# A four-layer fp32 kernel: in the last layer, image 0's depthwise convolution moved from TensorE to VectorE, setup work reordered, and another access pattern for the column products

## The chip, the core and the metric

The kernel runs on one core of a Trainium2 chip. The core has a matrix engine (TensorE, "PE" in the profile; its weight loads are "PEld"), a vector engine (VectorE, "DVE"), a scalar engine (ScalarE, "ACT"), a general engine (GpSimd, "POOL") and a queue engine that issues the DMAs used here (SyncE, "SP"). Compute tiles lie in SBUF, matmul results in PSUM, which this kernel treats as eight "banks" of 512 fp32 values per partition.

The metric is the device time of one execution in microseconds. The time before is the median of three runs. The profile is of one more execution; the span in it goes from the first to the last instruction.

## What is computed

Four layers follow one another on four images of 192 channels and 56 x 56 pixels, all in fp32. Only the last is touched. For each image it does, cut down:

```python
xn = layer_norm(x)                                # over channels
xc, z = split(in_proj_w @ xn)                     # 192 channels each
xc = silu(depthwise_conv3x3(xc, conv_w) + conv_b) # "u" in the kernel
xs = [rows(xc), columns(xc), reversed rows, reversed columns]
dts, Bv, Cv = split(x_proj_w[k] @ xs[k])          # 12 + 4 + 4 values per pixel, 4 directions
dt = softplus(dt_proj_w[k] @ dts + dt_proj_b)
h[t] = exp(dt*A) * h[t-1] + dt*Bv*xs              # a scan of 3136 pixels, 4 states per channel
y = sum over directions of (h . Cv) + Ds * xs
out = x + out_proj_w @ (layer_norm(y) * silu(z))
```

The first and third directions walk the image along rows, the second and fourth along columns, so the products `x_proj_w @ xs` are needed once in row order and once in column order.

## The kernel before

`layer3` is the last layer. Channels are held as two halves of 96 partitions, and an image as seven chunks of 448 pixels (eight rows). Tiles that feed matmuls have 128 partitions, and partitions 96 to 127 hold zeros. Its parts, by name:

- **Setup** (lines 1688 to 1753). Weights are loaded, the input bias is formed by 16 small matmuls (L1695) and copied (L1702), and the projection weights are scaled on DVE (L1704). An identity is made on POOL, and from it 18 diagonal matrices of 96 x 96, one for each tap of the 3 x 3 convolution and each half (L1722, DVE). `keep` allocates the working tiles and, where asked, zeroes partitions 96 to 127 on POOL (L1732): two u tiles, y, two pads, four rows, two sq; the dr tiles are zeroed whole (L1740). This part is placed by the framework's own scheduler.
- **`begin(b, c)`** starts chunk c of image b: loads x (L1803), prepares the borders of a padded tile on POOL (L1809 to L1815), normalizes (`layer_norm`: matmul L1768, DVE L1770, ACT square L1778, matmul L1783, ACT L1786 and L1787, DVE L1789), projects with matmuls (L1821) and writes the pad on ACT (L1832). The convolution then runs on PE: nine matmuls per half, each with one diagonal as weights and a shifted window of the pad as input, summed in a bank (L1851), and copied with its bias to u by ACT (L1859). The gate is projected and copied (L1868), both get SiLU (L1873, L1874), and `product` forms the row product. A chunk's pad work waits until the chunk before has its pad, and until the chunk before last is convolved.
- **`product`** is two matmuls into a bank (L1893), a copy by ACT (L1896) and a store (L1899). `begin_columns` calls it once per chunk of columns when all rows of the image are done, and there it reads u at a stride of 56 values: consecutive matmul columns are consecutive rows of the image.
- **`load`, `sizes`, `decay`, `scan`** do a step of 448 pixels of one direction. In `scan`, per half: DVE forms du (L2046 in row order, L2049 in column order), PE spreads it (L2056), DVE multiplies (L2062, three) and scans (L2078, three), POOL multiplies the states by C (L2085), PE sums over states (L2101), and DVE adds into y (L2106, L2111, L2115). L2115 reads the bank at a stride of 56 values and y in runs of eight.
- **`final(b, c)`** normalizes y, gates, projects and stores.

The order of these instructions on PE, DVE, ACT and POOL is fixed when the kernel is built: `Order.run` holds all the generators as threads, each with a place, and repeatedly takes the operation that could start first by assumed costs (`on_pe`, `on_dve`, ...), plus 0.05 times its place. Image 0's chunks have places -52 + 6c, steps have about 2t. A thread may yield a condition, and then it waits until the condition holds. Each engine runs its list strictly in order.

A fp32 matmul shows in the profile as two records. The third layer (`layer2`) has depthwise convolutions of its own, on DVE: one `tensor_scalar` and eight `scalar_tensor_tensor` operations per half (L1341, L1343).

Of the kernel before, what the change touches and what calls it, by code (L numbers as in the profile page):

```python
# [240 lines left out]
class Order:  # L241
# [20 lines left out]
    def take(self, kind="bank"):  # L262
        slot = min((s for s in self.kinds[kind] if s[0] is not None), key=lambda s: s[0])
        slot[0] = None
        return slot[1]

    def done(self, tile):

        (slot,) = (s for slots in self.kinds.values() for s in slots if s[1] is tile)
        slot[0] = self.end + self.LATENCY  # L270
# [66 lines left out]
def on_act(*n, takes=(), table=None, ready=None):  # L337
    return "ACT", sum(0.2 + 0.0009 * i for i in n), takes, table, ready
# [1337 lines left out]
def layer3(tc, src, packs, aps, dst):  # L1676
# [8 lines left out]
    with ExitStack() as ctx:  # L1685
# [28 lines left out]
        nc.vector.memset(eps, EPS)  # L1714

        ident = const.tile([HALF, HALF], F32, name="c_ident")
        make_identity(nc, ident)
        diag = const.tile([128, 2, 9, HALF], F32, name="diag")
        nc.gpsimd.memset(diag[HALF:], 0.0)
        for h in range(2):  # L1720
            for t in range(9):
                nc.vector.tensor_scalar_mul(diag[:HALF, h, t], ident, w["c96.conv_w"][:, h, t : t + 1])  # L1722

        per = ctx.enter_context(tc.tile_pool(name="c_per", bufs=1))
        ps = ctx.enter_context(tc.tile_pool(name="c_ps", bufs=1, space=PSUM))

        def keep(name, shape, n, rows=128, zero=True):

            tiles = [per.tile([rows, *shape], F32, name=f"{name}{i}") for i in range(n)]
            if zero:  # L1730
                for t in tiles:
                    nc.gpsimd.memset(t[HALF:], 0.0)  # L1732
            return tiles

        us = keep("u", [2, HW], 2)
        (y,) = keep("y", [2, HW], 1)
        pads = keep("pad", [2, 11, W + 2], 2)
        drs = keep("dr", [SCH], 3, zero=False)
        for t in drs:
            nc.gpsimd.memset(t, 0.0)  # L1740
        order = Order(
            nc,
            bank=[ps.tile([128, 512], F32, name=f"c_bank{i}") for i in range(8)],
            row=keep("row", [2, CH], 4),
            sq=keep("sq", [2, CH], 2),
            gate=keep("gate", [2, CH], 2, HALF, False),
            prod=keep("prod", [512], 2, 40, False),
            dr=drs,
            bc=keep("bc", [SCH], 8, zero=False),
            dt=keep("dt", [SCH], 6, HALF, False),  # L1750
            du=keep("du", [SCH], 3, HALF, False),
            da=keep("da", [SCH], 10, zero=False),
            st=keep("st", [SCH], 12, zero=False),
        )
        take, done = order.take, order.done
        prods = [[dram.tile([40, HW], F32, name=f"prod{b}_{o}") for o in range(2)] for b in range(B)]
# [35 lines left out]
        def begin(b, c):  # L1792


            u = us[b % 2]

            yield lambda: (b, c) == (0, 0) or (gone("begun", b, c - 1) if c else gone("begun", b - 1, NCHUNK - 1))
            yield lambda: b < 2 or gone("scanned", b - 2)

            yield lambda: b == 0 or gone("multiplied", 8 * NSC * (b - 1) + 4 * c)  # L1800
            yield on_sp("row", "row")
            xl, xn = take("row"), take("row")
            nc.sync.dma_start(xl[:HALF], pixels(src[b])[:, :, c * CH : (c + 1) * CH])  # L1803

            i = NCHUNK * b + c
            pad, above = pads[i % 2], pads[(i - 1) % 2]
            yield lambda: i < 2 or gone("convolved", i - 2)
            yield on_pool(200, 200)
            nc.gpsimd.memset(pad[:HALF, :, :, 0 : W + 2 : W + 1], 0.0)  # L1809
            if c == 0:  # L1810
                nc.gpsimd.memset(pad[:HALF, :, 1], 0.0)
            else:
                nc.gpsimd.tensor_copy(pad[:HALF, :, 0:2, 1 : 1 + W], above[:HALF, :, 8:10, 1 : 1 + W])
            if c == NCHUNK - 1:
                nc.gpsimd.memset(pad[:HALF, :, 10], 0.0)  # L1815
            yield from layer_norm(xl, xn, over=(xl,))

            def project(m):
                px = take()
                for k in range(2):  # L1820
                    nc.tensor.matmul(  # L1821
                        px[:HALF, :CH], inT[:, k, HALF * m : HALF * m + HALF], xn[:, k], start=(k == 0), stop=(k == 1)
                    )
                return px

            tiles = []
            for m in range(2):
                yield on_pe(2 * CH, "bank")
                tiles.append(project(m))
            for m in range(2):  # L1830
                yield on_act(CH)
                nc.scalar.activation(  # L1832
                    pad[:HALF, m, 2:10, 1 : 1 + W],
                    rows2(tiles[m][:HALF, :CH]),
                    AF.Identity,
                    bias=in_b[:, m : m + 1],
                )
                done(tiles[m])
            passed.add(("begun", b, c))
            y0, y1 = max(8 * c - 1, 0), 8 * c + (8 if c == NCHUNK - 1 else 7)  # L1840
            n = y1 - y0
            at = y0 - (8 * c - 1)
            px = slice(y0 * W, y1 * W)
            zt = None
            for h in range(2):
                pz = pc = None
                for t in range(9):
                    yield on_pe(n * W, *(("bank",) if t == 0 else ()), ready=order.end - 0.5 if t else None)
                    if t == 0:
                        pc = take()  # L1850
                    nc.tensor.matmul(  # L1851
                        rows2(pc[:HALF, : n * W]),
                        diag[:, h, t],
                        pad[:, h, at + t // 3 : at + t // 3 + n, t % 3 : t % 3 + W],
                        start=(t == 0),
                        stop=(t == 8),
                    )
                yield on_act(n * W)
                nc.scalar.activation(  # L1859
                    u[:HALF, h, px], pc[:HALF, : n * W], AF.Identity, bias=w["c96.conv_b"][:, h : h + 1]  # L1860
                )
                done(pc)
                yield on_pe(2 * CH, "bank")
                pz = project(2 + h)
                yield on_act(CH, takes=() if h else ("gate",))
                if h == 0:
                    zt = take("gate")
                nc.scalar.activation(zt[:, h], pz[:HALF, :CH], AF.Identity, bias=in_b[:, 2 + h : 3 + h])  # L1868
                done(pz)
            done(xn)  # L1870
            passed.add(("convolved", i))
            yield on_act(2 * n * W, 2 * CH, table=SILU)
            nc.scalar.activation(u[:HALF, :, px], u[:HALF, :, px], AF.Silu)  # L1873
            nc.scalar.activation(zt, zt, AF.Silu)  # L1874
            yield on_sp()
            nc.sync.dma_start(pixels(zmem[b])[:, :, c * CH : (c + 1) * CH], zt)
            done(zt)
            yield from product(b, 0, px, u[:, :, px], 2)
            passed.add(("rows", b, c))

        def begin_columns(b, c):
            yield lambda: all(gone("rows", b, i) for i in range(NCHUNK))
            uv = us[b % 2].rearrange("p h (y x) -> p h x y", x=W)[:, :, 8 * c : 8 * c + 8]
            yield from product(b, 1, slice(c * CH, (c + 1) * CH), uv, 4)
            passed.add(("columns", b, c))

        def product(b, o, px, u, passes):

            n = px.stop - px.start
            yield on_pe(passes * n, "bank")  # L1890
            pp = take()
            for k in range(2):
                nc.tensor.matmul(pp[:40, :n], w["c128.xpT"][:, k, o], u[:, k], start=(k == 0), stop=(k == 1))  # L1893
            yield on_act(n, takes=("prod",))
            t = take("prod")
            nc.scalar.copy(t[:, :n], pp[:40, :n])  # L1896
            done(pp)
            yield on_sp()
            nc.sync.dma_start(prods[b][o][:, px], t[:, :n])  # L1899
            done(t)  # L1900
# [225 lines left out]
        for b in range(B):  # L2126
            for c in range(NCHUNK):
                order.add(n * (b - 1) + 6 * c + 4, begin(b, c))
                order.add(n * (b - 1) + 48 + c, begin_columns(b, c))
                order.add(n * (b + 1) - 2 * c, final(b, c))  # L2130
        for t in range(len(steps)):
            order.add(2 * t - 5, load(t))
            if t % 2 == 0:
                order.add(2 * t - 3, sizes((t, t + 1)))
            for h in range(2):
                order.add(2 * t + h - 1, decay(t, h))
                order.add(2 * t + h, scan(t, h))
# [35 lines left out]
```

## Time and profile before

| what | value |
|---|---|
| median of three runs | 6957.4 us (6956.57 to 6957.86) |
| the profiled execution's own time | 6951.71 us |
| its span | 6949.9 us |
| mean granted PE clock | 0.931 of full speed |
| PE busy | 5890.7 us (85%) |
| DVE busy | 5908.5 us (85%) |
| ACT busy | 2640.6 us (38%) |
| POOL busy | 1423.8 us (20%) |
| last layer's first weight load is issued | at 4901.8 us |

A group line of the profile names the line, the engine, the operation, its output and inputs with sizes, and the count; after the bar come busy microseconds and the mean nanoseconds of one; after the next bar the engine's idle time before these instructions and what ended it. In the chain of waits, each line has a start, a length, and the work on the chain. In the table by stage, "granted clock" is the share of full speed that PE was given. A busy engine is only a bound where the others wait for it, so the last layer is read stage by stage below.

### The profile page before, as it was taken

The numbers are of one execution on the slowest core, as the hardware profiler recorded it, in microseconds if no ns is written. First come the engines' busy times: TensorE is split into PE (matmuls) and PEld (weight loads), VectorE is DVE, ScalarE is ACT, GpSimd is POOL, SyncE is SP. The second block draws the span as 40 slices with busy tenths as digits, with TensorE's granted clock in tenths as the row PEclk, the third lists the DMA queues.
The fourth block names the chain that finished last, engine by engine and source line by source line (L and its number), as shares of the span: only waits on it lengthen the run. The fifth ranks groups of instructions, "written<-read, shape, count | busy, mean of one in ns | idle before, by whom it ended". The sixth has DMA issues, their size and how long they took to land. (4 is left out here: it accounts for less than half of the span.)

```text
span 6949.9 us, 107660 instructions
## 1 busy us (share of the span) xinstructions
PE 5890.7 (85%) x43810; PEld 2685.0 (39%) x43810; DVE 5908.5 (85%) x7379; ACT 2640.6 (38%) x4083; POOL 1423.8 (20%) x1409
## 2 busy tenths in 40 slices
PE   4999979999999994968888787885799989899776
PEld 2445434444444441345444444442332222222211
DVE  2799999999999999648999898997348788887897
ACT  1111112221122211135555455543256656556543
POOL 0000000000000000032222222220125445445564
PEclk9999989999999997979999899987899999999998
DMA  3222112221222112110000000000145555555654
GB/s 94 56 52 64 34 35 53 58 65 35 52 64 61 35 45 73 45 52 16 19 19 14 19 17 17 19 14 8 34 104 130 142 143 129 152 133 136 166 151 108
DMA packets 252044, 462.69 MB, mean 67 GB/s; under 512 B 30388, under 2 KB 237964, under 8 KB 240412
## 3 DMA queue, kind: packets, MB, share of 16 engines
q1 hardware_dynamic: 251548, 455.80, 25.8%
q8 instruction: 345, 5.65, 0.3%
q14 instruction: 151, 1.24, 0.1%
HBM read 238.58 MB, written 62.96 MB: 43 GB/s over the span
## 5 line engine op out<-in xcount | busy, mean ns | idle before, releaser
L789 DVE TENSOR_TENSOR pr<-vdx,attn 112x1792 f32<-112x1792 f32 (+4 forms) x720 | 1185.6, 1648 | 19.0
L634 PE MATMUL a_bank<-qk_in,w_a 64*49 64x392 f32 x9408 | 1156.3, 496 | 0.0
L2085 POOL TENSOR_TENSOR da<-st,bc 128x448 f32<-128x448 f32 x672 | 859.0, 1283 | 862.9 <-DVE st L2078 618.9
L794 DVE TENSOR_TENSOR oa<-oa,pr 112x1792 f32<-112x1792 f32 (+1 forms) x423 | 764.8, 1808 | 0.0
L634 PE MATMUL a_bank<-qk_in,wd 64*49 64x392 f32 x4032 | 689.6, 493 | 0.0
L2078 DVE TENSOR_TENSOR_SCAN st<-da,st,c_bank 128x448 f32<-128x448 f32 x576 | 646.6, 1132 | 0.0
masks.py:197 POOL MEMSET b_ident<- 128x128 f32 x1 | 0.2, 205 | 2856.0 <-DVE sc L1042 2856.0
L634 PEld LDWEIGHTS a_bank<-qk_in,w_a 64*49 64x49 f32 x9408 | 431.6, 120 | 394.1 <-issue 389.2
L2062 DVE TENSOR_TENSOR c_bank<-c_bank,bc 128x448 f32<-128x448 f32 x672 | 382.5, 618 | 153.1 <-PE c_bank L2056 152.5
L315 ACT ACT_TABLE_LOAD x378 | 485.0, 1283 | 6.6
L2031 ACT ACTIVATE da<-da,a_neg 128x448 f32<-128x448 f32 x672 | 414.1, 658 | 122.5 <-DMA da<-dt 117.9
L1343 DVE SCALAR_TENSOR_TENSOR bg<-bzpad,w_b,bg 128x448 f32<-128x448 f32 (+2 forms) x672 | 423.1, 684 | 0.0
L2101 PE MATMUL c_bank<-da,w_c 128*32 128x448 f32 x1344 | 349.5, 570 | 66.3 <-POOL da L2085 61.4
L1851 PE MATMUL c_bank<-pad,diag 128*96 128x448 f32 (+2 forms) x1008 | 396.8, 543 | 2.4 <-ACT pad L1832 2.3
L794 DVE TENSOR_TENSOR ob<-ob,pr 112x1792 f32<-112x1792 f32 (+3 forms) x282 | 393.0, 1394 | 0.0
L2056 PE MATMUL c_bank<-du,w_c 32*128 32x448 f32 x1344 | 257.8, 624 | 121.6 <-DVE du L2046 80.4
L869 PE MATMUL a_bank<-xc,w_a 128*128 128x448 f32 x672 | 296.8, 571 | 66.0 <-DVE xc L854 66.0
L878 ACT ACTIVATE hm<-a_bank,w_a 128x448 f32<-128x448 f32 x168 | 106.4, 634 | 637.4 <-PE a_bank L869 618.3
L634 PEld LDWEIGHTS a_bank<-qk_in,wd 64*49 64x49 f32 x4032 | 247.4, 119 | 256.5 <-issue 254.6
L1432 PE MATMUL bank<-bxn,w_b 128*128 128x448 f32 (+2 forms) x672 | 288.1, 557 | 24.8 <-DVE bxn L1215 18.6
L884 PE MATMUL a_bank<-hm,w_a 128*96 128x448 f32 x672 | 290.6, 564 | 21.3 <-ACT hm L878 21.3
L655 PE MATMUL a_bank<-qk_sum,w_a 64*49 64x168 f32 (+1 forms) x5376 | 277.7, 337 | 27.1 <-DVE qk_sum L625 25.2
(305 smaller groups left out, 9825.2 us busy)
## 6 DMA issues: line engine op xcount, KB each, us to landing
da<-dt SPq DMA_DIRECT2D x672, 224.0 KB
vdx<-vmem SPq DMA_DIRECT2D x168, 476.0 KB
bc<-prod SPq DMA_DIRECT2D x224, 224.0 KB
row<-x SPq DMA_DIRECT2D x56, 336.0 KB
x<-x SPq DMA_DIRECT2D x4, 2352.0 KB
vmem<-vt SPq DMA_DIRECT2D x56, 168.0 KB
xc<-x SPq DMA_DIRECT2D x56, 168.0 KB
mid<-xc SPq DMA_DIRECT2D x56, 168.0 KB
```

The costliest lines, as they stand in the source:

```text
L315: self.nc.scalar.preload_act_table_set(table)
L634: nc.tensor.matmul(py[a][outs[g], : 7 * W].rearrange("p (y x) -> p y x", x=W), wt[halves[a], dx], q[halves[a], r, i0 + m : i0 + m + 7, dx ...
L789: nc.vector.tensor_mul(pr, vv, wt)
L794: nc.vector.tensor_add(og, og, before)
L869: nc.tensor.matmul(ph[:, :CH], w["a128.c1T"][:, k, 128 * m : 128 * m + 128], xt[:, k], start=(k == 0), stop=(k == 1),)
L1343: nc.vector.scalar_tensor_tensor(dst, x, wt[:, t : t + 1], dst, ALU.mult, ALU.add)
L1851: nc.tensor.matmul(rows2(pc[:HALF, : n * W]), diag[:, h, t], pad[:, h, at + t // 3 : at + t // 3 + n, t % 3 : t % 3 + W], start=(t == 0), ...
L2031: nc.scalar.activation(da, da, AF.Exp, scale=a_neg[:, k, g : g + 1])
L2062: nc.vector.tensor_mul(tiles[j][:, :SCH], tiles[j][:, :SCH], b_)
L2078: nc.vector.tensor_tensor_scan(sts[j][:, r], da[:, r], tiles[j][:, :SCH][:, r], first, ALU.mult, ALU.add)
L2085: nc.gpsimd.tensor_mul(da, sts[j], c_)
L2101: nc.tensor.matmul(py[32 * j : 32 * j + 32, :SCH], w["c128.sum"], das[j], start=True, stop=True)
```

## The change

Five things change, all in `layer3`:

1. Image 0's convolution is done on DVE: per half, one `tensor_scalar` (tap 0 times weight, plus bias) and eight `scalar_tensor_tensor` operations that add a tap each, straight into u. Its matmuls and the ACT copy with bias are not issued. Images 1 to 3 keep the matmuls.
2. The 18 diagonals are built by a thread of their own, `diagonals`, with place 0, once the row product of image 0's fourth chunk has been placed; later images' convolutions wait for it, in the written order.
3. The zeroing is shared: the row, sq and pad tiles are zeroed on DVE; u, dr, the diagonals' lower rows and y on POOL, in that order, with the identity made after dr.
4. The column products read u in image-row order: for each row, eight neighbouring values. The result is written to the bank at a stride of 56 values, so the bank's content is laid out as before.
5. The planner's cost of a column product goes from 4 to 2 passes.

```diff
+        rows = keep("row", [2, CH], 4, zero=nc.vector)
+        sqs = keep("sq", [2, CH], 2, zero=nc.vector)
+        pads = keep("pad", [2, 11, W + 2], 2, zero=nc.vector)
+        us = keep("u", [2, HW], 2, zero=nc.gpsimd)
+        drs = keep("dr", [SCH], 3)
         for t in drs:
             nc.gpsimd.memset(t, 0.0)
+        make_identity(nc, ident)
+        nc.gpsimd.memset(diag[HALF:], 0.0)
+        (y,) = keep("y", [2, HW], 1, zero=nc.gpsimd)
...
-                pz = pc = None
-                for t in range(9):
+                pz = pc = uh = None
+                if b == 0:
+
+                    for t in range(9):
+                        yield on_dve(n * W, each=0.0012, ready=order.end - 0.3 if t else None)
+                        v = pad[:HALF, h, at + t // 3 : at + t // 3 + n, t % 3 : t % 3 + W]
+                        uh = rows2(u[:HALF, h, px])
+                        wt = w["c96.conv_w"][:, h, t : t + 1]
+                        if t == 0:
+                            nc.vector.tensor_scalar(uh, v, wt, w["c96.conv_b"][:, h : h + 1], ALU.mult, ALU.add)
+                        else:
+                            nc.vector.scalar_tensor_tensor(uh, v, wt, uh, ALU.mult, ALU.add)
+                if uh is None:
+                    yield lambda: gone("diagonals")
+                for t in range(9 if uh is None else 0):
...
-                yield on_act(n * W)
-                nc.scalar.activation(
-                    u[:HALF, h, px], pc[:HALF, : n * W], AF.Identity, bias=w["c96.conv_b"][:, h : h + 1]
-                )
-                done(pc)
+                if uh is None:
+                    yield on_act(n * W)
...
+        def diagonals():
+
+            yield lambda: gone("rows", 0, 3)
+            for h in range(2):
+                for t in range(9):
+                    yield on_dve(HALF)
+                    nc.vector.tensor_scalar_mul(diag[:HALF, h, t], ident, w["c96.conv_w"][:, h, t : t + 1])
+            passed.add(("diagonals",))
+
         def begin_columns(b, c):
             yield lambda: all(gone("rows", b, i) for i in range(NCHUNK))
-            uv = us[b % 2].rearrange("p h (y x) -> p h x y", x=W)[:, :, 8 * c : 8 * c + 8]
-            yield from product(b, 1, slice(c * CH, (c + 1) * CH), uv, 4)
+            uv = us[b % 2].rearrange("p h (y x) -> p h y x", x=W)[:, :, :, 8 * c : 8 * c + 8]
+            yield from product(b, 1, slice(c * CH, (c + 1) * CH), uv, 2)
...
+            out = pp[:40, :n].rearrange("p (x y) -> p y x", y=H) if o else pp[:40, :n]
             for k in range(2):
-                nc.tensor.matmul(pp[:40, :n], w["c128.xpT"][:, k, o], u[:, k], start=(k == 0), stop=(k == 1))
+                nc.tensor.matmul(out, w["c128.xpT"][:, k, o], u[:, k], start=(k == 0), stop=(k == 1))
...
+        order.add(0, diagonals())
```

More of the change, by code (lines that the diff above doesn't have):

```diff
@@ L1716, in layer3, with keep @@
         ident = const.tile([HALF, HALF], F32, name="c_ident")
-        make_identity(nc, ident)
         diag = const.tile([128, 2, 9, HALF], F32, name="diag")
-        nc.gpsimd.memset(diag[HALF:], 0.0)
-        for h in range(2):
-            for t in range(9):
-                nc.vector.tensor_scalar_mul(diag[:HALF, h, t], ident, w["c96.conv_w"][:, h, t : t + 1])
         per = ctx.enter_context(tc.tile_pool(name="c_per", bufs=1))
         ps = ctx.enter_context(tc.tile_pool(name="c_ps", bufs=1, space=PSUM))
-        def keep(name, shape, n, rows=128, zero=True):
+        def keep(name, shape, n, rows=128, zero=None):
             tiles = [per.tile([rows, *shape], F32, name=f"{name}{i}") for i in range(n)]
@@ L1731, in keep @@
                 for t in tiles:
-                    nc.gpsimd.memset(t[HALF:], 0.0)
+                    zero.memset(t[HALF:], 0.0)
             return tiles
[L1735 to L1738, printed above, removed]
+        rows = keep("row", [2, CH], 4, zero=nc.vector)
[3 more added lines that the diff above has]
+        drs = keep("dr", [SCH], 3)
         for t in drs:
             nc.gpsimd.memset(t, 0.0)
+        make_identity(nc, ident)
+        nc.gpsimd.memset(diag[HALF:], 0.0)
+        (y,) = keep("y", [2, HW], 1, zero=nc.gpsimd)
         order = Order(
@@ L1743, in layer3 @@
             bank=[ps.tile([128, 512], F32, name=f"c_bank{i}") for i in range(8)],
[L1744 to L1747, printed above, removed]
+            row=rows,
+            sq=sqs,
+            gate=keep("gate", [2, CH], 2, HALF),
+            prod=keep("prod", [512], 2, 40),
             dr=drs,
[L1749 to L1753, printed above, removed]
+            bc=keep("bc", [SCH], 8),
+            dt=keep("dt", [SCH], 6, HALF),
+            du=keep("du", [SCH], 3, HALF),
+            da=keep("da", [SCH], 10),
+            st=keep("st", [SCH], 12),
         )
@@ L1845, in begin @@
             for h in range(2):
-                pz = pc = None
-                for t in range(9):
+                pz = pc = uh = None
[12 more added lines that the diff above has]
+                for t in range(9 if uh is None else 0):
                     yield on_pe(n * W, *(("bank",) if t == 0 else ()), ready=order.end - 0.5 if t else None)
@@ L1857, in begin @@
                     )
-                yield on_act(n * W)
-                nc.scalar.activation(
-                    u[:HALF, h, px], pc[:HALF, : n * W], AF.Identity, bias=w["c96.conv_b"][:, h : h + 1]
-                )
-                done(pc)
+                if uh is None:
+                    yield on_act(n * W)
+                    nc.scalar.activation(
+                        u[:HALF, h, px], pc[:HALF, : n * W], AF.Identity, bias=w["c96.conv_b"][:, h : h + 1]
+                    )
+                    done(pc)
                 yield on_pe(2 * CH, "bank")
```

## The prediction

> **What bounds the kernel now.** I read five views in this order. First the page's engine totals: TensorE 85% and VectorE 85% of the span, so neither is the bound throughout and the stages must be looked at apart. Second, busy time by stage of the last layer:
>
> ```profile
> 4904.00:4940.00 36.00, 11.76 (x29) 5.81 (x30) 26.09 (x25) 4.93 (x7) 25.82 (x17) 0.55 0.19 56
> 4942.00:5118.00 176.00, 173.38 (x475) 68.53 (x474) 26.78 (x32) 81.30 (x113) 10.67 (x20) 1.00 0.23 61
> 5118.00:5153.00 35.00, 32.78 (x62) 6.43 (x63) 17.14 (x22) 12.48 (x18) 10.84 (x9) 0.95 0.25 70
> 5153.00:6455.00 1302.00, 1175.09 (x3843) 363.63 (x3844) 1039.09 (x1341) 787.08 (x1123) 631.75 (x521) 0.96 0.55 138
> 6455.00:6950.00 495.00, 349.79 (x1098) 90.31 (x1097) 438.80 (x565) 239.37 (x350) 273.42 (x208) 0.89 0.54 141
> ```
>
> After the stage and its length come the busy microseconds of PE, its weight loads, DVE, ACT and POOL, then PE's granted clock. While image 0 is begun (4942 to 5118) PE is busy 98% and DVE 15%. From 5153 to 6455, where each image's scans run beside the next image's convolution, PE has 90%, DVE 80%. The last image's scans are DVE's (89%). Third, the chain of waits:
>
> ```profile
> 4904.00 10.70 POOL u L1732 x2
> 4914.70 5.38 POOL y L1732
> 4924.15 3.74 POOL row L1732 x4
> 4927.89 1.60 POOL sq L1732 x2
> ...
> 5003.19 6.77 PE c_bank L1851 x18
> 5009.95 4.51 PE c_bank L1821 x12
> 5014.46 6.06 PE c_bank L1851 x16
> 5020.52 1.63 PE c_bank L1893 x4
> ...
> 5129.79 23.19 PE c_bank L1893 x28
> ```
>
> Three things lead to image 0's scans: POOL's zeroing (L1768 starts at 4926.24, during the row memsets), the convolution L1851, about 13.7 of each chunk's 25.3 us (L1768 starts at 4972.50, 4997.78, 5023.07), and the column products: seven take 23.19 us, 3.31 each, where a row product takes 1.63 for the same 448 columns. Fourth, the groups by line give DVE's prices (busy total, mean):
>
> ```profile
> L1343 DVE SCALAR_TENSOR_TENSOR bxn<-bapad,w_b,bxn 96x448 f32<-96x448 f32 x320 | 207.6, 689 | 0.0
> L1341 DVE TENSOR_SCALAR bxn<-bapad,w_b 96x448 f32<-96x448 f32 x40 | 19.1, 516 | 0.0
> L2111 DVE TENSOR_TENSOR y<-y,c_bank 96x448 f32<-96x448 f32 x56 | 34.0, 607 | 14.8 <-PE c_bank L2101 14.5
> L2115 DVE TENSOR_TENSOR y<-y,c_bank 96x448 f32<-96x448 f32 x112 | 68.1, 608 | 93.7 <-PE c_bank L2101 93.5 <-ACT da L2031 0.2
> ```
>
> L1343 and L1341 are layer 2's own depthwise convolution, the same operations on windows of the same shape. Fifth, the timeline of 4904 to 5160, for starts and ends.
>
> **Part 1, the start.** Removed ahead of L1768: 18 diagonal products on DVE (21.04 us at 4904, stretched by POOL: the longest, 5.41, has the length of a u memset) and POOL's memsets of y, pad, row and sq ahead of or in the way of the first chunk. Added on DVE: the row, sq and pad memsets, 3.74 + 1.60 + 2.44 = 7.8 us by POOL's rows. DVE is free from 4901.8 and L1712 took its 0.14 us inside a POOL memset, so I expect no stretching: done by 4912. Then L1768 waits for PE's own queue: the bias products L1695 end at 4913.0, after the weights land at 4910.2. L1768 at 4913.0 against 4926.24: **-13 us**. POOL keeps u 10.70, dr 1.53, identity 0.43, diag 1.53, y 5.38 = 19.6, to 4923.6; the pad edges behind them (0.5) end at 4924.1, ahead of the first pad write at 4939.93 - 13 = 4926.7. That cover is 2.6 us; what exceeds it comes on the path. L1704's two products can be held by u's memset to 4914.7; needed at 4924. SP's queue is unchanged; the first rows were loaded by 4912.
>
> **Part 2, image 0's convolution.** PE loses 14 half-chunks, 7 x 13.7 = 96 us, all on the chain; ACT loses 14 L1859 copies (0.63 each, 9 us, hidden). DVE gains 14 x (0.52 + 8 x 0.64) = 79 us; 0.64 lies between L1343's start-to-start 0.60 and mean 0.69. Behind each such instruction queue the next chunk's L1770 and L1789, for which PE's L1783 and L1821 wait: one operation, 0.6 us a time. Summing DVE's work until the state that before has at 5153:
>
> - convolution 79; the norms of six chunks and of image 1's first (L1770 and L1789): 7 x 2.15 = 15;
> - the five half-steps of scans done by then: each du 0.6, three multiplications 1.7, three scans 3.3, one sum 0.67, about 6.5, so 33;
> - the diagonals, now after image 0's fourth chunk: 18, between 0.15 (estimate from 96 elements at L1711's rate) and 1.2 each (L1722 under POOL). POOL is then mostly idle; I take 0.4, 7 us.
>
> That is 134 us. The first pad is ready at 4940.6 - 13 = 4927.4, so a DVE that never idles ends at 5061. It will idle: a chunk's chain of L1768, L1770, L1778, L1783, L1786, L1789, L1821, L1832 took 11.8 us unloaded (4972.5 to 4984.3), may start only when the chunk before last is convolved, and the last image-0 chunk is followed by SiLU and its product (4 us) before any column product. L2046, which like L1343 reads two tiles of SBUF, has a mean of 0.846 against 0.589 at best while POOL is half busy; here POOL has 15 products of 1.28 in some 130 us, so perhaps 0.08 for each of 112 operations, 9 us, of which 0.64 holds 4. For all this I allow 10%, 13 us: 5074, or 79 us earlier than 5153. The column products of image 0 (Part 3) run beside this DVE work on an otherwise light PE, so their own saving is partly in it; I add 5. Parts 1 and 2: **-84 us** (bounds -100, DVE never idle, and -45, the slower chunk of rival B).
>
> Later images: their convolution stays on PE and additionally waits, in the written order, for the diagonals. They are queued near 5000 to 5040, image 1's convolution follows after 5050: nothing. The new condition shifts the planner's places a little; +-10 us in the range.
>
> **Part 3, column products.** Their input u is now read in runs of eight contiguous values, the bank is written at a stride of 56 values. If the read alone sets the price, a product falls from 3.31 to 1.63: 1.68 x 21 = 35 us of PE for images 1 to 3. PE is 90% busy there and DVE fell to 37 of 50 us in the windows with the products (40 elsewhere), so I take 70%: **-24 us**. The trace has no matmul with a strided bank. The nearest row is L2115 against L2111: DVE reads the bank at just this stride and y in just these runs, and pays 0.608 against 0.607. [...] The bounds are 1.63 and, a guess with no row behind it, 8. I take the row, because a matmul here delivers a value per 0.84 ns and record and DVE drew strided ones at 1.36 ns: at that pace a product would still cost only 2.4.
>
> **Sum.** -84 - 24 = -108 against the profiled execution's 6951.71 (span 6949.9 and 1.8 around it): 6844. The timed median, 6957.4, is 5.7 higher, so **6850**.
>
> **Rivals.**
> A. *The bank's stride eats the column gain* (3.31 as before): 6850 + 29 = 6879. [...]
> B. *Image 0's chunks are bound by the chain, not by DVE's work.* PE will now have gaps. At the start, 33% busy, it had a clock of 0.55, and L1768, L1783 and L1821 took 3.27, 3.18 and 4.94 instead of 1.67, 1.74 and 3.2: 4.8 us a chunk, 29 us for six chunks, plus 10 for DVE's order: 6889. [...]
> C. *Slower.* The strided bank costs far more than the strided read. With A and Parts 1 and 2 the gain left is 79; each extra microsecond per product costs 7 + 0.7 x 21 = 22 us, so it decides from 3.31 + 3.6 = 6.9 us per product on; at 8 it is 6980. L2115 speaks against; nothing in the trace excludes it.
> D. *No change*: the planner's new order loses in 5153 to 6455 what the start gained, because both PE and DVE are near full. Against: the order there comes from the same costs, except for the columns. 6957.
>
> **How the numbers follow.** Chances: forecast 0.62, A 0.13, B 0.13, C 0.07, D 0.05. The forecast's own range is 6815 to 6880 (DVE never idle and all 35 us: 6957 - 16 - 11 - 108 = 6822; the planner's 10 below). A and B reach to about 6905. I give 6810 to 6905, which leaves C, D and some tails out. A measurement of this kernel tells 0.2%, 14 us: faster 0.88 (forecast, A, B), same 0.04, slower 0.08.
>
> **What would show it.** L1768 first at about 4913; the first L1832 near 4927; some 126 DVE operations of 0.5 to 0.65 us on u, DVE about 90% and PE about 75% busy to 5050; chunks 15 to 17 us apart instead of 25; L1893 at 0.41 us a record for columns as for rows; the first image-1 convolution some 80 us earlier; PE's busy sum some 140 us lower. Wrong would be: L1893 records of 0.8 us or more, PE's clock below 0.8 in that stage, or a distance from the first image-1 convolution to the end that has grown.

## The result

| | before | after |
|---|---|---|
| median of five runs, us | 6957.86 (6956.57 to 6960.48) | 6850.14 (6844.28 to 6855.94) |
| ratio | | 0.9845 (95%: 0.9831 to 0.9858) |
| profiled execution, its span | 6951.71, 6949.9 | 6850.6, 6848.8 |
| last layer in it | 2048.5 | 1939.8 |

"Last layer" runs from its first instruction on DVE, the memset of c_ones at L1711, to the end. The layers ahead of it, which the change doesn't touch, took 4901.4 us in one profile and 4909.1 in the other, so below the last layer is compared by times counted from that memset. It is 108.8 us shorter. In the changed kernel the convolution's lines on DVE are L1855 (first tap) and L1857 (the other eight), PE's convolution is L1864, the product L1918 (before: L1893), and the zeroing L1727.

| us after that memset | before | after | gained so far |
|---|---|---|---|
| first mean, L1768 on PE | 24.9 | 11.9 | 13.0 |
| first subtraction, L1770 on DVE | 28.2 | 24.0 | 4.2 |
| first pad write, L1832 on ACT | 38.5 | 33.6 | 4.9 |
| last column product of image 0, its end | 251.6 | 192.0 | 59.6 |
| first convolution matmul of image 1 | 258.5 | 198.9 | 59.6 |
| end | 2048.5 | 1939.8 | 108.8 |

So 60 us come before image 1's convolution and 49 behind it. The page's engine totals of the changed kernel:

```profile
PE 5770.1 (84%) x43558; PEld 2650.3 (39%) x43558; DVE 5982.6 (87%) x7513; ACT 2621.1 (38%) x4063; POOL 1409.3 (21%) x1401
```

Busy time by stage of its last layer, with the columns as before (stage, length, then busy time of PE, weight loads, DVE, ACT and POOL, then PE's granted clock):

```profile
4942.00:5060.00 118.00, 88.85 (x208) 30.52 (x206) 97.83 (x149) 68.93 (x93) 9.47 (x16) 0.88 0.30 81
5100.00:5400.00 300.00, 278.68 (x949) 91.44 (x947) 233.84 (x301) 185.49 (x264) 144.06 (x121) 0.99 0.54 131
5400.00:6360.00 960.00, 842.28 (x2882) 267.00 (x2882) 798.44 (x1034) 592.27 (x852) 484.87 (x399) 0.96 0.58 145
6360.00:6850.00 490.00, 358.65 (x1114) 92.58 (x1112) 438.66 (x571) 237.86 (x350) 274.87 (x209) 0.89 0.56 145
```

While image 0 is begun, DVE is busy 83% and PE 75%: neither is full, and PE's clock fell from 1.00 to 0.88. Images 1 and 2 (5400 to 6360) have PE at 88% and DVE at 83%. The chain of waits in the first stage shows one chunk, and then the column products:

```profile
4949.26 1.09 DVE row L1770
4950.36 0.96 ACT sq L1778
4951.37 3.30 PE c_bank L1783 x4
4954.67 2.39 PE c_bank L1821 x4
4957.73 1.28 ACT L315
4959.03 0.86 ACT u L1887
4959.88 0.84 ACT gate L1888
4961.89 0.79 DVE u L1857
4967.60 1.09 DVE row L1770
...
5090.38 10.65 PE c_bank L1918 x28
```

From one L1770 to the next the chain runs through the norm and the projection, past a table load and both SiLUs on ACT, into one half's taps. The seven column products take 10.65 us where they took 23.19.

### The profile page after: what moved, and what is told of

Its sections match the earlier page's. It is cut to its first block, busy times and chain, and to the rows that moved or that the text cites. A ratio compares the mean times of both kernels' runs of the same rounds, so it can differ in the third digit from the quotient of the medians.

```text
span 6848.8 us, 107270 instructions
## 1 busy us (share of the span) xinstructions
PE 5770.1 (84%) x43558; PEld 2650.3 (39%) x43558; DVE 5982.6 (87%) x7513; ACT 2621.1 (38%) x4063; POOL 1409.3 (21%) x1401
## 4 chain that ended last, share of the span: by engine, by line
DVE 49%; PE 35%; issue 7%; ACT 5%; DMA 2%; POOL 2%; SPq 0%; DVEq 0%; POOLq 0%; ACTq 0%
DVE pr L789 9%; DVE oa L794 7%; PE a_bank L634 6%; DVE bg L1343 5%; DVE ob L794 4%; PE c_bank L1864 4%; DVE st L2103 3%; DVE bxn L1343 3%; PE c_bank L1821 2%; PE a_bank L869 2%; PE a_bank L884 2%; PE c_bank L2081 2%; PE c_bank L2126 2%; DVE c_bank L2087 2%; PE bank L1506 1%
## 5 line engine op out<-in xcount | busy, mean ns | idle before, releaser
L586 ACT ACTIVATE qk_in<-a_bank,qk_bias,qk_scale 64x224 f32<-64x224 f32 (+5 forms) x288 | 146.1, 525 | 420.8 <-PE a_bank L571 418.5
L1864 PE MATMUL c_bank<-pad,diag 128*96 128x448 f32 (+2 forms) x756 | 297.4, 543 | 2.3 <-ACT pad L1832 2.3
```

The costliest lines, as they stand in the source:

```text
L1864: nc.tensor.matmul(rows2(pc[:HALF, : n * W]), diag[:, h, t], pad[:, h, at + t // 3 : at + t // 3 + n, t % 3 : t % 3 + W], start=(t == 0), ...
```

## The experiments

Every time below is a median. Each kernel was timed beside runs of the kernel before, and the ratio is to those. "Columns end" is the end of image 0's last column product, counted as in the table above, and "last layer" its length, both in the one profiled execution. The layers ahead, which no kernel here changes, took 4901.4 to 4918.7 us in these 14 profiles, so single times can differ by some 17 us for reasons that lie ahead of `layer3`.

| run | time, us | ratio (95%) | columns end | last layer |
|---|---|---|---|---|
| before | 6957.9 | 1 | 251.6 | 2048.5 |
| e6: planner's cost alone | 6938.4 | 0.9970 (0.9959 to 0.9981) | 251.7 | 2028.7 |
| e2: all but the columns | 6905.5 | 0.9923 (0.9906 to 0.9939) | 204.5 | 1994.5 |
| e1: the columns alone | 6893.2 | 0.9910 (0.9895 to 0.9924) | 239.2 | 1981.1 |
| e5: the change with cost 4 | 6884.2 | 0.9894 (0.9878 to 0.9911) | 192.0 | 1974.0 |
| e4: halves' taps in turn | 6867.8 | 0.9873 (0.9859 to 0.9888) | 210.3 | 1956.8 |
| e10: e9 with cost 1 | 6853.7 | 0.9851 (0.9837 to 0.9866) | 185.4 | 1943.4 |
| e7: in turn, norm in between | 6850.9 | 0.9844 (0.9830 to 0.9859) | 183.5 | 1939.7 |
| the change | 6850.1 | 0.9845 (0.9831 to 0.9858) | 192.0 | 1939.8 |
| e9: e3 and e8 together | 6848.4 | 0.9844 (0.9827 to 0.9860) | 185.4 | 1936.1 |
| e3: a_neg on ACT | 6846.1 | 0.9841 (0.9827 to 0.9856) | 187.0 | 1929.7 |
| e8: filler matmuls | 6840.3 | 0.9832 (0.9817 to 0.9846) | 186.9 | 1933.1 |
| e11: next norm first | 6839.7 | 0.9834 (0.9819 to 0.9849) | 173.5 | 1936.5 |
| e12: e11, e3 and e8 | 6833.9 | 0.9821 (0.9805 to 0.9838) | 170.2 | 1927.4 |

My theory was the prediction's: DVE's work sets the first stage, TensorE's saved time the rest. The rivals to tell apart were that the first stage is bound by the chain of a chunk (rival B, with a lower clock of PE), and that the planner's new order, not TensorE's saved time, makes the gain of the columns.

**e1, the columns alone.** To the kernel before are added the new access and the cost:

```diff
-            uv = us[b % 2].rearrange("p h (y x) -> p h x y", x=W)[:, :, 8 * c : 8 * c + 8]
-            yield from product(b, 1, slice(c * CH, (c + 1) * CH), uv, 4)
+            uv = us[b % 2].rearrange("p h (y x) -> p h y x", x=W)[:, :, :, 8 * c : 8 * c + 8]
+            yield from product(b, 1, slice(c * CH, (c + 1) * CH), uv, 2)
...
+            out = pp[:40, :n].rearrange("p (x y) -> p y x", y=H) if o else pp[:40, :n]
```

> The kernel before with only the column products changed (read of u in runs of eight, bank at a stride of 56, planner's cost 2 passes); image 0's convolution stays on TensorE and the zeroing is as before. The prediction's Part 3: L1893-type records for columns at 0.38 us, image 0's seven products leave the chain at 23.2 - 11.7 us, images 1 to 3 give 24 us of their 35: about 36 us faster, 6922. Theory 'the column change is worth more than its own TensorE time' (after image 0's columns the changed kernel gained 49 us where Part 3 said 24): 12 + 49 = 61 us faster, 6897. Rival 'the surplus comes from the other edits': 36 or less.

Measured 6893.2, 65 us less than before. PE's groups by shape, of the kernel before and then of e1:

```profile
L1893 PE MATMUL c_bank<-u,w_c 128*40 128x448 f32 x192 | 132.5, 830 | 0.5
```

```profile
L1894 PE MATMUL c_bank<-u,w_c 128*40 128x448 f32 x192 | 82.2, 565 | 0.8
```

After the bar are the busy total and the mean nanoseconds. TensorE saves 50 us in all four images, and the gain is 65: the columns bring more than the engine's own saving.

**e2, all but the columns.** The changed kernel, with these lines of e1 back in their old form.

> The changed kernel with the column products as they were before (read of u at a stride of 56 values, contiguous bank, planner's cost 4 passes). By the prediction's sum the column edit gave 24 + 5 of the 108 us: this is at 6850 + 29 = 6879. If the edit is worth more than its TensorE time, 6850 + 50 to 60 = 6900 to 6910. The stage up to image 0's columns keeps its gain of about 60 us, less what its own columns lose (up to 12).

Measured 6905.5, 52 us less than before and 55 more than the change. The columns of image 0 end 47.1 us earlier than before (251.6 - 204.5), and this lead reaches the end with some 5 us more. The start and the moved convolution are therefore worth 52 us together, not the forecast's 79 (84 less its 5 us of image 0's columns). By the marks of this run 4.9 us are won at the first pad write and 42 between it and the columns' end; no run has the new setup or the moved convolution alone.

**e5 and e6, the planner's cost alone.** In e5 the change keeps its access but tells the planner 4 passes; in e6 the kernel before keeps its access but tells 2.

```diff
-            yield from product(b, 1, slice(c * CH, (c + 1) * CH), uv, 2)
+            yield from product(b, 1, slice(c * CH, (c + 1) * CH), uv, 4)
```

> The changed kernel with only the planner's cost of a column product put back to 4 passes (1.7 us assumed for a product by its new price, 3.4 by its old one); access and work as changed. The column edit as a whole was worth 55 to 65 us in the two runs before, TensorE's own saving in it is 4 x 11.7 = 47. Theory 'the rest is the planner's order': this loses 10 to 18 us, 6860 to 6868. Rival 'the rest is TensorE's time too, passed on by more than its share': 6846 to 6854, no loss.

> The kernel before with only the planner's cost of a column product changed from 4 to 2 passes; the products themselves stay slow (3.31 us). Theory 'the order is worth 10 to 18 us by itself': 6940 to 6948. Rival 'a cost below the true one makes the planner pack work that then waits': 6957 or slower. If neither order costs anything, 6957 and the column edit's 55 to 65 us are all matmul time.

Measured 6884.2 and 6938.4: the loss in e5 is larger than its theory's 10 to 18 us, the gain in e6 just above them. The four combinations on the kernel with the moved convolution and on the kernel before:

| | from | to | us |
|---|---|---|---|
| new access, cost left at 4 | e2 6905.5 | e5 6884.2 | -21 |
| cost 4 to 2, new access | e5 6884.2 | change 6850.1 | -34 |
| cost 4 to 2, old access | before 6957.9 | e6 6938.4 | -20 |
| new access, cost at 2 | e6 6938.4 | e1 6893.2 | -45 |

The figure 2, which moves no data and saves no instruction, is worth 20 to 34 us, and without it the new access is worth half. By images, from one image's last column product to the next and then to the end, e5 has 349.9, 467.6, 467.6 and 496.9 us, and the change 329.8, 456.5, 457.6 and 503.9: the change is 20, 11 and 10 us shorter in the first three and 7 longer in the last. In the first of them PE ran some 1100 records in e5 and 1045 in the change, so part of the 20 us is work that only lay ahead of the mark. Over the last layer PE runs the same 5252 records in both, and is busy 1624.0 us in e5 and 1606.8 in the change: half of the 34 us is idle time of PE, half is longer busy time for the same records. What in the order makes this was not isolated.

**e3, the sign change on ACT.** One operation of the setup moves:

```diff
-        nc.vector.tensor_scalar_mul(a_neg, a_neg, -1.0)
+        nc.scalar.activation(a_neg, a_neg, AF.Identity, scale=-1.0)
```

DVE's timeline of the changed kernel (start, length) shows why:

```profile
4920.68 0.16 DVE L1702 COPY in_b<-pb 96x4 f32<-96x4 f32 x1 [5.03 <-PE pb L1695]
4920.76 2.31 DVE L1704 TENSOR_SCALAR w_c<-w_c,w_c 96x384 f32<-96x384 f32 x2
4923.30 0.81 DVE L1727 MEMSET sq<- 32x896 f32 x1 [0.22 <-issue]
4924.12 5.19 DVE L1707 TENSOR_SCALAR a_neg<-a_neg 128x24 f32<-128x24 f32 x1
4929.53 0.81 DVE L1727 MEMSET sq<- 32x896 f32 x1 [0.22 <-issue]
4930.55 1.12 DVE L1727 MEMSET pad<- 32x1276 f32 x1 [0.22 <-issue]
4931.89 1.12 DVE L1727 MEMSET pad<- 32x1276 f32 x1 [0.21 <-issue]
4933.04 1.08 DVE L1770 TENSOR_TENSOR row<-row,c_bank 96x896 f32<-96x896 f32 x1
```

and POOL's:

```profile
4923.95 5.32 POOL L1727 MEMSET y<- 32x6272 f32 x1
```

L1707 works on 24 values per partition and takes 5.19 us: it begins 0.17 us after POOL's memset of y and ends with it. Behind it in DVE's list are one sq and both pads, and only then L1770, whose mean PE had ready at 4924.2.

> The changed kernel with one instruction moved: the sign change of a_neg (L1707) runs on ScalarE behind the exponential that makes a_neg, not on VectorE. Theory 'L1707 held by GpSimd's memset of y ate the start's gain': L1770 first starts about 5 us earlier counted from the c_ones memset (24.0 us there in the changed kernel, 19 here), and the whole is about 5 us faster, 6845. Rival 'the weights and TensorE's first matmuls set that start': L1770 stays at 24 and the time at 6850.

L1770 came 18.7 us after the first memset instead of 24.0, the first pad write 29.9 instead of 33.6, and the columns ended 5.0 us earlier. The time, 6846.1, is 4 us lower, within what these runs can tell. What L1707 costs at the start is shown, 5.3 us; its worth at the end is not: 4 us by the medians, 10 by the last layer of the one profile.

**e4, the halves' taps in turn.** Image 0's taps alternate between the two halves, so that no operation reads what the one before it wrote:

```diff
-            for h in range(2):
-                pz = pc = uh = None
-                if b == 0:
-                    for t in range(9):
+            uh = None
+            if b == 0:
+                for t in range(9):
+                    for h in range(2):
```

> The changed kernel with image 0's taps in another order: tap 0 of half 0, tap 0 of half 1, tap 1 of half 0, and so on, so that no operation reads what the one ahead of it wrote. Theory 'a dependent chain pays about 0.1 us per operation' (start to start 0.717 in the changed kernel's chains of 96x448, 0.60 to 0.64 in layer 2, which alternates): start to start falls to 0.60 to 0.64, 112 operations save 9 to 13 us of VectorE, and the whole is 5 to 12 us faster unless the gate's projections, which now come behind both halves, cost it. Rival 'the duration is that of the windows and GpSimd': start to start stays at 0.71 and the time within 4 us of 6850.

DVE's timeline of the changed kernel, and then of e4, in like chunks:

```profile
4967.60 1.08 DVE L1770 TENSOR_TENSOR row<-row,c_bank 96x896 f32<-96x896 f32 x1
4968.60 0.50 DVE L1855 TENSOR_SCALAR u<-pad,w_c 96x448 f32<-96x448 f32 x1
4969.14 5.70 DVE L1857 SCALAR_TENSOR_TENSOR u<-pad,w_c,u 96x448 f32<-96x448 f32 x8
4974.76 1.08 DVE L1789 TENSOR_TENSOR row<-row,c_bank 96x896 f32<-96x896 f32 x1
4979.06 0.51 DVE L1855 TENSOR_SCALAR u<-pad,w_c 96x448 f32<-96x448 f32 x1 [3.22 <-ACT pad L1832]
4979.60 5.70 DVE L1857 SCALAR_TENSOR_TENSOR u<-pad,w_c,u 96x448 f32<-96x448 f32 x8
4985.22 1.07 DVE L1770 TENSOR_TENSOR row<-row,c_bank 96x896 f32<-96x896 f32 x1
```

```profile
4969.94 1.07 DVE L1770 TENSOR_TENSOR row<-row,c_bank 96x896 f32<-96x896 f32 x1
4976.57 1.08 DVE L1789 TENSOR_TENSOR row<-row,c_bank 96x896 f32<-96x896 f32 x1 [5.56 <-ACT c_bank L1787]
4982.41 1.16 DVE L1854 TENSOR_SCALAR u<-pad,w_c 96x448 f32<-96x448 f32 x2 [4.75 <-ACT pad L1832]
4983.49 9.61 DVE L1856 SCALAR_TENSOR_TENSOR u<-pad,w_c,u 96x448 f32<-96x448 f32 x16
4993.02 1.07 DVE L1770 TENSOR_TENSOR row<-row,c_bank 96x896 f32<-96x896 f32 x1
```

Sixteen taps took 9.61 us, 0.60 each, where eight that depend on one another took 5.70, 0.71 each. Yet the chunk grew from 17.6 us (4967.60 to 4985.22) to 23.1 (4969.94 to 4993.02) and the kernel from 6850 to 6868: all eighteen taps now stand ahead of the next L1770, and DVE waits 5.56 and 4.75 us with nothing to do. In both kernels a chunk is the chain from L1770 to the taps' start plus the taps ahead of the next L1770: 4979.06 - 4967.60 = 11.5 and one half's 6.2 in the change, 4982.41 - 4969.94 = 12.5 and both halves' 10.6 in e4. DVE's total doesn't enter. That is rival B's chain, though by DVE's order and only partly by PE's clock.

**e7, in turn, with the next norm in between.** e4, with breaks after the first rounds of taps in which the planner may place the next norm, the condition for the next chunk's pad met right after the taps, and e3's edit:

```diff
+                        at_ = order.end + (0.5 if h == 0 and t >= 2 else -0.3)
+                        yield on_dve(n * W, each=0.0012, ready=at_ if t or h else None)
...
+                passed.add(("convolved", i))
```

> The changed kernel with three edits for image 0: halves alternate tap by tap, a break after each pair of taps lets the next chunk's norm into VectorE's list in the middle of a chunk's taps, the chunk counts as convolved when its taps are placed, and a_neg's sign is changed on ScalarE. Theory 'what sets image 0's chunks is where the next norm stands in VectorE's list': L1770 and L1789 now have taps behind them, taps start every 0.60 us, the distance of chunks falls from 17.5 to some 14 or 15 us, and with 5 us from the start the whole is 20 to 30 us faster than the changed kernel: 6820 to 6830. Rival 'TensorE's clock and the chain of eight operations bound the chunk': distance stays at 17 or more, 6840 to 6850.

Measured 6850.9, as the change. DVE's timeline:

```profile
4964.29 1.07 DVE L1770 TENSOR_TENSOR row<-row,c_bank 96x896 f32<-96x896 f32 x1
4965.29 4.84 DVE L1857 SCALAR_TENSOR_TENSOR u<-pad,w_c,u 96x448 f32<-96x448 f32 x8
4970.26 1.08 DVE L1789 TENSOR_TENSOR row<-row,c_bank 96x896 f32<-96x896 f32 x1
4971.26 1.27 DVE L1857 SCALAR_TENSOR_TENSOR u<-pad,w_c,u 96x448 f32<-96x448 f32 x2
4978.88 0.51 DVE L1855 TENSOR_SCALAR u<-pad,w_c 96x448 f32<-96x448 f32 x1 [6.34 <-ACT pad L1832]
```

The taps are at 0.60 each and hide most of the norm, and then DVE idles 6.34 us for the next pad write. The chunk is still a chain (14.6 us from L1770 to the next taps) plus what stands ahead of the next L1770 (5.1). Chunks of 448 pixels start 17.4 to 19.7 us apart, not 14 or 15. Faster taps and earlier norms within one chunk only moved the idle time.

**e8, a busier PE.** Four matmuls per chunk of image 0 are added behind the first gate projection, ahead of the next chunk's variance matmul L1783; they write rows 96 to 127 of a bank, which nothing reads:

```diff
+                if b == 0 and h == 0:
+                    for k in range(4):
+                        nc.tensor.matmul(pz[HALF:, :CH], ones[:, :32], xn[:, k % 2], start=True, stop=True)
```

> The changed kernel with four extra matmuls per image-0 chunk, into unused partitions of a bank that is open anyway, placed ahead of L1783 where TensorE otherwise waits over 4 us: nothing is added to the chain but TensorE's gap is filled, so its clock should stay near 1.0 in that stage and L1783 take 1.74 instead of 3.2 us. Rival B of the prediction, that TensorE's lower clock (0.86 there) lengthens the chunks: 10 us faster or more, 6840. Theory 'VectorE's list sets the chunk': L1789 stands behind the second half's taps anyway, so within 4 us of 6850.

The stage in e8, to be read against the first line of the change's table:

```profile
4942.00:5060.00 118.00, 100.58 (x269) 33.12 (x267) 102.98 (x157) 72.68 (x97) 12.82 (x20) 0.97 0.32 83
```

PE's timeline of the change and of e8, at the same L1783:

```profile
4951.37 3.30 PE L1783 MATMUL c_bank<-sq,c_ones 128*96 128x448 f32 x4 [4.24 <-ACT sq L1778]
```

```profile
4948.69 1.74 PE L1783 MATMUL c_bank<-sq,c_ones 128*96 128x448 f32 x4 [1.12 <-ACT sq L1778]
```

With 4.24 us of idle time ahead of it L1783 took 3.30 us, with 1.12 us it took 1.74. The granted clock rose from 0.88 to 0.97, the chunks went from 17.6 to 17.0 us, and the time to 6840.3. The clock is a real part of the chunk's length.

**e9 and e10, the two edits together, and a still lower cost.** e9 is e3 with e8; e10 is e9 with 1 pass.

> The changed kernel with both edits that gained by themselves: the sign change of a_neg on ScalarE (-4 us alone) and four added matmuls per chunk of the first image's projection (-10 us alone), which write into rows of a bank that the next projection overwrites anyway. Theory: the early end of the first image's columns is carried to the end when it comes from the start and from the clock, so the two add up: columns end some 5 us earlier than with the added matmuls alone (near 181 us after the layer's start) and the time is 6834 to 6842. Rival: both shorten the same stretch, and what lies behind it (the planner's order of images 1 to 3) sets the end; then the time stays at 6840 to 6850 although the columns end earlier.

> The same kernel, and the planner's cost of a column product lowered once more, from 2 passes to 1 (the code of the products is as in the changed kernel). Lowering it from 4 to 2 was worth 20 us on the kernel before and 34 us on top of the new access. Theory: the gain came from the order that TensorE's work gets when the planner's figure is near what the product takes (448 columns for two halves at 0.38 us are 0.76 us; 2 passes of 448 columns are told to the planner as 1.7 us, 4 as 3.4 us, and 1 as 0.85 us, nearest to the truth): 5 to 15 us faster than the same kernel with 2 passes, 6820 to 6835. Rival: the planner's order moves the time in either direction without regard to how near its figure is: within 10 us of the other, or slower by up to 20.

e9 measured 6848.4: the two gains did not add, and by the rival that I had put there nothing of them is left. In its profile the last layer is 3.6 us shorter than the change's (1936.1) though the columns end 6.6 us earlier. So differences of 10 us between single variants (e8 against e9) are not to be explained one by one: I keep for the clock a worth of 0 to 10 us. e10 came out 5 us above e9, within what the runs can tell, and not 5 to 15 below. But its expectation had a product's time wrong: 0.76 us is half of it. A product is four records of 0.38 us, and seven take 10.65 us, 1.52 each, so with the new access 2 passes, told as 1.7 us, are already the nearest figure, and 1 pass, 0.85 us, is farther off. It is e6 that speaks against nearness: with the old access a product takes 3.31 us, 4 passes are told as 3.4, and the farther figure 2 gained 20 us all the same.

**e11, the next norm first.** By e4's reading a chunk shortens when the next L1770 no longer stands behind a half's taps. In e11 the norm of chunk c+1 is begun before the taps of chunk c, which wait for its place in the list; the pad's edges follow the norm:

```diff
+            if b == 0:
+                yield from layer_norm(xl, xn, over=(xl,), read=("subtracted", c))
+                passed.add(("normed", b, c))
+                yield lambda: c == 0 or gone("begun", b, c - 1)
...
+                    yield lambda: c == NCHUNK - 1 or gone("subtracted", c + 1)
                     for t in range(9):
```

> The changed kernel, with the norm of image 0's chunk c+1 begun, up to its subtraction L1770, ahead of the taps of chunk c (the pad's edges then follow the norm). Theory: in the changed kernel a chunk lasts as long as its chain from L1770 to the second pad write, 11.6 us, plus one half's taps, 6.2 us, because L1770 of the next chunk stands behind the first half's taps in DVE's list: 17.7 us. With L1770 ahead of them, a chunk lasts as long as DVE's own work: two halves of 6.27 and 2.15 for L1770 and L1789, 14.7 us. Chunks then start 14.7 to 15.5 us apart, the columns of image 0 end 12 to 17 us earlier (175 to 180 us after the layer's start, with 192 in the changed kernel). If what is gained there is carried to the end, 6833 to 6840. Rival: TensorE's low clock makes each link of the chain longer, and chunks stay at 16.5 us or more. Second rival: the columns end earlier as said, but the end of the kernel is set by what comes behind, and the time stays within 6 us of 6850.

DVE's timeline of e11:

```profile
4968.99 1.07 DVE L1770 TENSOR_TENSOR row<-row,c_bank 96x896 f32<-96x896 f32 x1
4969.99 0.50 DVE L1862 TENSOR_SCALAR u<-pad,w_c 96x448 f32<-96x448 f32 x1
4970.53 5.70 DVE L1864 SCALAR_TENSOR_TENSOR u<-pad,w_c,u 96x448 f32<-96x448 f32 x8
4977.08 1.08 DVE L1789 TENSOR_TENSOR row<-row,c_bank 96x896 f32<-96x896 f32 x1 [0.85 <-ACT c_bank L1787]
4978.08 0.50 DVE L1862 TENSOR_SCALAR u<-pad,w_c 96x448 f32<-96x448 f32 x1
4978.62 5.70 DVE L1864 SCALAR_TENSOR_TENSOR u<-pad,w_c,u 96x448 f32<-96x448 f32 x8
4984.70 1.08 DVE L1770 TENSOR_TENSOR row<-row,c_bank 96x896 f32<-96x896 f32 x1 [0.38 <-PE c_bank L1768]
```

The idle time of a chunk is down to 1.2 us. Chunks with 448 pixels start 15.7, 15.7, 14.8 and 15.5 us apart (4968.99, 4984.70, 5000.44, 5015.27, 5030.81), and the columns end at 173.5, where 175 to 180 was expected. The time is 6839.7, 10 us below the change (6837.1, 6838.2, 6841.2 and 6857.0; the profile is of the last, in which the layers ahead took 4918.7 us and PE's clock from 5450 to 6360 was 0.95, with 4909.1 and 0.97 in the change's). The theory of the chunk holds. By the medians about half of the 18.5 us reach the end; in this profile the last layer is only 3 us shorter than the change's.

**e12, e11 with e3 and e8.**

> The same, with the sign change of a_neg on ScalarE (the first chunk 4 to 5 us earlier) and the four added matmuls per chunk (a higher clock). Theory: chunks 14.7 us apart, columns end at 170 to 174 us after the layer's start, some 20 us earlier than in the changed kernel; carried to the end that is 6828 to 6834, and by the two edits' earlier joint result (7 us earlier at the columns, 2 us in the time) rather 6838 to 6844. Rival: nothing of it reaches the end, 6845 to 6855.

Measured 6833.9 (6832.4 to 6837.8), the fastest of all: 16 us below the change and 124 below the kernel before. Its slowest run lies below the change's fastest, 6844.3. The chunks are 15.1 to 16.5 us apart, where 14.7 was expected. The columns end at 170.2, 22 us earlier than in the change; of these 16 arrive.

## Why the prediction came out at the right time

The forecast was 6850, with 84 us for Parts 1 and 2 and 24 for Part 3. The time is 6850.14, but the sum was right by luck, through two errors of opposite sign:

| term of the sum | forecast | measured |
|---|---|---|
| Parts 1 and 2, without image 0's columns | -79 | -52 (e2 against before) |
| columns, all images | -29 | -55 (the change against e2) |

Of the 55 us 12.5 are image 0's columns (their end at 204.5 in e2, 192.0 in the change), for which I had 5, and some 42 the rest, for which I had 24.

**Part 1, the start: its first half right, its end wrong.** L1768 came 11.9 us after the first memset; the step, 4913.0 - 4901.4, said 11.6. The failed sentence is "DVE is free from 4901.8 ... so I expect no stretching: done by 4912". The sq and pad memsets do not lie ahead of L1702 in DVE's list but behind it and L1704, and all but one sq behind L1707 too, and L1702 waits for PE until 11.6 us after the first memset. L1770 then stood at 24.0 us instead of 14.9 (11.6 and the 3.3 from L1768 to L1770 of before); 5.3 of these 9.1 us are L1707's hold, by e3, and the rest is DVE's list. I had weighed a hold by POOL's memsets for L1704 alone, not for every `tensor_scalar` in the list. In the trace L1707 took 5.19 us beside POOL's memset of y (5.32), while DVE's four row memsets took 0.81 us each beside POOL's memsets of u, as long as the sq memset at 4929.53, behind POOL's. Why the one was held and the others were not, no run shows. The gain at the first pad write was 4.9, not 13, and the cover of 2.6 us for POOL's pad edges was not tested: they ended at 4929.8, 13 us before the first pad write.

**Part 2, the convolution: the work right, the limit wrong.** From the first pad write to the columns' end DVE was busy 132 us, where I had 134. The taps were dearer (85.5 us for 79; 0.71 each on 448 pixels, where each reads what the one before wrote, and 0.60 in e4, where none does), the diagonals as said (6.3 us for 7), the rest cheaper. But the stretch lasted 158.4 us, not 146.6: DVE was idle 26 us, where I had allowed 13. The step that failed is the limit, DVE's summed work with 10% on it; "chunks 15 to 17 us apart" was 17.4 to 22.3 behind the first. The idle time lies mostly where a chunk's list holds little but its own taps and norms: some 16 us in the gaps up to 5016, and 6 at the end, behind 5088. Between them, with scans and diagonals in the list, no gap is over 0.2 us, and DVE's summed work was the right limit for the chunks of 20.1 and 22.3 us. I had listed the links of a chunk's chain, 11.8 us, and used them only as a reason for the 10%. Chain plus one half's taps, 11.5 + 6.2, gives 17.7, and the chunks without scans were 17.6 and 17.4. e11, which takes the tap block out of the chain, needs 139.9 us from the first pad write to the columns' end, within the forecast's 146.6: DVE's sum with an allowance fits e11's order, not the change's.

**Rival B** had 0.13. Its mechanism was there: L1783 took 3.30 us, its records in that stage had a median of 951 ns where before had 539, and the clock was 0.88. In the changed kernel gaps of 3.14 to 4.61 us stand ahead of L1783 from image 0's second chunk to its last, and behind five of the six it took 3.10 to 3.30 us, behind the other, of 3.36, 2.04; behind 1.12 us in e8 it took 1.74. I had set against it the stage 6455 to 6950 of before, PE 71% busy at a clock of 0.89, and an estimate of some 4 us from it: the 29 us times (1/0.89 - 1) / (1/0.55 - 1). A stage's mean clock says little of the matmul behind a gap: at 0.88, L1783 took 3.30 us for 1.74. By e8 and e9 the worth is 0 to 10 us, of B's 29.

**Part 3, the columns: the price right, the gain nearly twice the forecast.** A column product costs what a row product does: PE's group of the changed kernel, to be read against L1893 of before,

```profile
L1918 PE MATMUL c_bank<-u,w_c 128*40 128x448 f32 x192 | 81.4, 560 | 0.8
```

and 28 records in 10.65 us, 0.38 each, so 1.52 a product, where a row product of before took 1.63. The bank's stride costs nothing here (56 fp32 values, 448 columns, u read in runs of eight). The row L2115 against L2111 was the right guide. Rivals A, with 3.31 us a product, and C, with 8, a guess that no run shows, fall with the 1.52. What failed is "I take 70%" of 35 us, and "the planner's places a little; +-10 us in the range": I had counted only PE's saved time, and the cost of 2 passes alone brings 20 to 34 us (e6, e5). I had this number in the diff and gave it no step of its own. What images 1 to 3 pass on of PE's 35 us depends on it: at cost 4 the new access brought 21 us, of which 12.5 are image 0's columns, so some 9 came from the others; at cost 2 it brought 45, of which again 12.5 (251.7 - 239.2), so some 33. Rival D, a worse order, was the same effect with the wrong sign.

**PE's busy sum** was to fall by some 140. Over the last layer's PE groups it fell from 1800.0 to 1658.3, by 141.7, and over the whole page by 120.6, mostly because PE had been 17 us busier in the layers ahead in that execution. The distance from image 1's first convolution to the end was to shrink by 24 and shrank by 49 (1790.0 to 1740.9).

## What to carry to other kernels

When work moves to an idle engine, don't stop at the sum of that engine's work: also write down the list of one period, find what stands ahead of the operation that begins the next period's chain, and add the two. Where a planner fixes the order, its cost figures are part of the change, and are to be tried alone, on the old code too. A total that comes out right says nothing of its terms; undo the parts one by one.

## What the runs showed that I had not expected

- A DVE `tensor_scalar` of 128 x 24 values (L1707) took 5.19 us beside a POOL memset of 5.32, while DVE's memsets did not lengthen so: the four of 32 x 896 on the rows took 0.81 us each beside POOL's memsets of u, and in e3, next to the same memset of y, the two on sq took 1.75 for both and one on a pad 1.12, as in the change without it.
- `scalar_tensor_tensor` on 96 x 448 fp32 started every 0.71 us where it read what the one before wrote (the change), and every 0.60 where it did not (e4).
- fp32 matmuls that write a bank at a stride of 56 values ran at 0.38 us a record (28 in 10.65), as contiguous ones did (L1851 of before, 18 in 6.77); those of before that read SBUF at that stride had 0.83 (28 in 23.19).
- Four added matmuls per chunk made others faster: the stage's clock went from 0.88 to 0.97 and L1783 from 3.30 to 1.74 us, at no cost in time.
